# Two fused layers on one core: later residual updates, a longer first stretch for half 0, lists for the first unit, and transposes that nothing reads

## The chip, the cores and the metric

The kernel runs on one core of one Trainium2 chip. The metric is device time in microseconds (us) for one execution, smaller is better. The times stated for the kernel before are the median and range of three runs. One more execution was taken by the hardware profiler: its own time, and the span from its first to its last instruction, stand beside the three runs below, and all durations in this text are from it.

## The reference, cut to what matters

The input is 4 sequences of 256 tokens with 512 features, in float32. Four residual blocks follow one another, each on a layer norm of the running x:

```
x = x + retention(layernorm(x))     # 32 query heads, 8 key heads of 128, chunks of 128 tokens, decay, rms norm, gate, Wo
x = x + router(layernorm(x))        # 64 experts, softmax, top 8, mix of bias rows
x = x + state_space(layernorm(x))   # 8192 channels, conv of 4 taps, 128 heads, 8 groups, gate, rms norm per group, out_proj
x = x + adapters(layernorm(x))      # 64 adapters of rank 16, top 16
```

In the state space block each of the 8 groups g gives a sum over its 1024 channels that is multiplied, per token, by the group's own reciprocal root mean square r before it is added to x. So that sum is built in an accumulator (`acc`) and added to x when r is known: x = x + acc * r. That addition is called the residual update here (`settle`, L889).

## The kernel before, in words

The 1024 tokens are eight tiles of 128, four to a "half". Everything is done by half, so that one half can be in one block while the other is in another. A float32 product is made of three matmuls on a high and a low part (`hi`, `lo`) of each operand; a projection (`proj`, L199) is 12 such matmuls with 512 columns. Every weight block of 512 KB is loaded by SP into one of two `raw` buffers, then copied to its high part by ACT (L140), and its low part is made by POOL (L145). `Weights.until(n)` does this up to weight n in the program's order; otherwise it happens where a weight is first used.

Retention runs in 32 units (four heads' worth of queries in pairs, one half each). A unit's steps are written as a list of letters, one list for the first unit (`FIRST1`), one for most (`STEP1`), one while a block of the other half is worked on beside it (`SIDE1`). S is scores (L399), D the decays of the next unit (L384), F and C the two parts of the output product of the unit before (`finish`, L455), K, Q and G the next unit's keys, queries and gates, U the silu, A the product with the values and the squares (L414, L426), N the transposes and the gate (L440), P and T a piece of side work, and W a weight step, which does nothing in this block because `due` is -1 there. Steps marked by `k.line` keep their order on TensorE.

The state space block works on pairs of channel blocks: 8 groups of 4 pairs for each half. Each iteration i treats three pairs: the inputs of the next (B, I, G, X, D), the transposes and mixers of the present (T, M; L791, L814), and the output product of the one before (O, L865), which adds a PSUM bank into `acc` on VectorE (L885). The PSUM tag "o" of the output product has two banks. The order of pairs is: the first `FIRST3 * NC // 2` = 4 pairs of half 0, the same 4 of half 1, then pair by pair half 0 and half 1, and in the end two of half 0 and two of half 1. While half 0 does its first pairs, the router (L607) and the preparation of half 1 (L699: layer norm, time steps, cumulative sums, in `steps_of`, L212) are side work, one piece at each P or E. Before half 1 is first needed, what is left of it is emitted at once (L935). At the last pair of a group `scale` (L851) makes r with four matmuls, VectorE and POOL, and `settle` follows each of the four outputs at once (L886).

The program text gives each instruction a priority; a planner that simulates the engines makes each engine's order from it. `k.behind` forbids one order without a semaphore (an instruction is issued after another on the same engine). `keep_in_program_order` keeps one in its place; `LATE` names the weights whose high copy is so kept.

Of the kernel before, what the change touches and what calls it, by code (L numbers as in the profile page):

```python
# [11 lines left out]
F32 = mybir.dt.float32  # L12
F32R = mybir.dt.float32r
AF = mybir.ActivationFunctionType
ALU = mybir.AluOpType
# [3 lines left out]
P = 128  # L19
# [5 lines left out]
EPS = 1e-5  # L25
GONE = -30000.0
YB = 3
LONE1, FIRST3, LONE3 = 3, 1, 2
PUMP = 1
AHEAD = 0  # L30
BANK1, BANK3 = "o", "x"
LATE = (0, 3)
FIRST1 = "U S0 S1 S2 K Q0 W Q1 K A0 A1 W K G0 N0 W G1 N1 D E W".split()
STEP1 = "S0 D F S1 S2 K Q0 W Q1 K A0 A1 U W K C W P G0 N0 W G1 N1 E P W".split()
SIDE1 = "S0 D F P S1 S2 T K Q0 P W Q1 T K A0 A1 U W K C P P W G0 P N0 W G1 N1 E P W".split()
STEP3 = "W T0 T1 B I0 W M0 M1 X0 X1 I1 O0 G0 W W O1 W W P O2 W W G1 P W O3 D0 D1 W W".split()
# [3 lines left out]
SIDE3 = "T0 T1 I0 I1 M0 M1 P B X0 X1 P P O0 W O1 G0 G1 W W P O2 O3 W P W P D0 D1 E E".split()  # L40

# [40 lines left out]
def moments(k, tc, t, tag):  # L82

    nc = tc.nc
    stats = k.small([P, 6], f"stats_{tag}_{t}", "ln_stats")
    nc.vector.bn_stats(stats, k.x[t])
# [18 lines left out]
def turned(k, tc, xn, name):  # L105

    ps = k.psum.tile([P, KC, P], F32, tag=k.bank, name=f"ps_{name}")
    for c in range(KC):
        k.line(tc.nc.tensor.transpose(ps[:, c, :], xn[:, c * P:(c + 1) * P], k.ident))
    return ps  # L110


def normalize(k, tc, half, tag, into=("xn",)):


    nc = tc.nc
    tiles = [HT * half + at for at in range(HT)]
    of = [moments(k, tc, t, tag) for t in tiles]
    ahead = len(into)
    xns = [centre(k, tc, tiles[at], of[at], tag, into[at]) for at in range(ahead)]  # L120
    yield
    for at, t in enumerate(tiles):
        xn = xns[at]
        ps = turned(k, tc, xn, f"xn_{tag}_{t}")
        hi, lo = (part[:, :, at * P:at * P + P] for part in k.xs[half])
        nc.scalar.copy(hi, ps)
        nc.vector.tensor_tensor(lo, ps, hi.bitcast(F32), ALU.subtract)
# [182 lines left out]
def retention(k, tc, io, arrive, begun, done, tail):  # L310
# [5 lines left out]
    with ExitStack() as st:  # L316
# [35 lines left out]
        def rope(ps, hi, lo, name):  # L352
            ps = ps.rearrange("p (b s) -> p b s", b=2)
            t1 = k.wk.tile([P, 2, SEQ], F32, tag="cv", name=f"r1_{name}")
            one = nc.vector.tensor_tensor(t1, ps, mid(cos, 2), ALU.mult)
            if name == "k_0_0":

                tc.keep_in_program_order(one)
            t2 = k.wk.tile([P, 2, SEQ], F32, tag="xd", name=f"r2_{name}")
            nc.vector.tensor_tensor(t2[0:64], ps[64:128], mid(sin[64:128], 2), ALU.mult)  # L360
            nc.vector.tensor_tensor(t2[64:128], ps[0:64], mid(sin[0:64], 2), ALU.mult)  # L361
# [3 lines left out]
            nc.vector.tensor_tensor(lo, t1, hi.bitcast(F32), ALU.subtract)  # L365

        def keys(g, half, w):

# [30 lines left out]
        def scores(u, blk):  # L399

            kh, kl = u.kk
            zj, zi = ((0, 0), (1, 1), (0, 1))[blk]
            ps = k.psum.tile([P, 4, P], F32, tag="y", name=f"ps_sc_{u.name}_{blk}")
            for b in range(2):
                aj = slice((2 * b + zj) * P, (2 * b + zj) * P + P)
                ai = slice((2 * b + zi) * P, (2 * b + zi) * P + P)
                for i, (a, q) in enumerate(((kh, 0), (kh, 1), (kl, 0))):
                    k.line(nc.tensor.matmul(
                        ps[:, b::2, :], a[:, aj], qs[:, q, :, ai], start=(i == 0), stop=(i == 2)
                    ))  # L410
# [98 lines left out]
        for i in range(-1, len(units) + 1):  # L509
# [50 lines left out]
            def value(z):  # L560
# [111 lines left out]
def state_space(k, tc, io):  # L672
# [4 lines left out]
    NC = 8  # L677
# [136 lines left out]
    def mixer(p, n):  # L814
        nm, ch, xs, m, xd = f"{p.name}_{n}", p.ch + n, p.xs[n], p.m[n], p.xd[n]
        ps_y = k.psum.tile([P, HT, P], F32, tag="y", name=f"ps_y_{nm}")
        for b in range(2):
            for z, terms in ((0, ((0, 0),)), (1, ((0, 2), (1, 1)))):
                for i, (zs, blk) in enumerate(terms):
                    for h in range(2):  # L820
# [44 lines left out]
    def output(p, t):  # L865
# [17 lines left out]
            nc.scalar.copy(a, ps)  # L883
        else:
            nc.vector.tensor_tensor(a, a, ps, ALU.add)  # L885
        if p.cp == NC // 2 - 1 and p.g < NG - 1:  # L886
            settle(p, t)

    def settle(p, t):  # L889
        xt, a = k.x[HT * p.half + t], acc[p.g, p.half][:, t, :]  # L890
        one = nc.vector.scalar_tensor_tensor(xt, a, p.r[:, t:t + 1], xt, ALU.mult, ALU.add)
# [30 lines left out]
    def run(done):  # L922


        with tc.tile_pool(name="s3", bufs=1, reuse_waits="tile") as own.only:
            for i in range(-1, len(pairs) + 1):
# [16 lines left out]
                    output(before, t)  # L943

                def ended():
                    if before.half == 1:
                        scale(before)
                    for t in range(HT):
                        settle(before, t)
                    k.hold = own.exp if before.half == 0 else None  # L950
                    done(before.half)

                step = dict(
                    B=shared, I=lambda n: inputs(after, n), G=lambda n: gate(after, n),
# [179 lines left out]
def tile_two_layers(ctx: ExitStack, tc: tile.TileContext, io: dict, out: bass.AP):  # L1134
# [47 lines left out]
    def line(ins):  # L1182
# [5 lines left out]
        k.front = []  # L1188
        k.done = ins

    k.act, k.small, k.pump, k.behind, k.line = act, small, pump, order, line
    k.n, k.follow, k.done, k.main, k.root = 0, None, None, None, None
    k.rooted = None
    k.front = []
    k.hold = k.scaled = k.turned = None
    k.const = ctx.enter_context(tc.tile_pool(name="const", bufs=1))
    k.smalls = ctx.enter_context(tc.tile_pool(name="smalls", bufs=3))
    k.dram = ctx.enter_context(tc.tile_pool(name="dram", bufs=1, space=bass.MemoryType.DRAM))
# [110 lines left out]
```

## Time and profile before

| what | value |
|---|---|
| median of 3 runs (lowest to highest) | 2538.18 us (2537.22 to 2538.46) |
| the profiled execution's own time | 2536.5 us |
| its span, first to last instruction | 2534.7 us |
| mean granted TensorE clock | 0.987 |
| TensorE busy, retention alone, 254 to 381 us | 124.98 of 127 us |
| TensorE busy, start, 0 to 127 us | 100.81 of 127 us |
| TensorE busy, entry of the state space block, 889 to 1016 us | 106.41 of 127 us |
| the same, 1016 to 1143 us | 112.64 of 127 us |
| TensorE busy, both halves interleaved, 1143 to 2341 us | 1186.85 of 1198 us |

How to read it: PE is TensorE, DVE VectorE, ACT ScalarE, POOL GpSimd, SP the engine that issues DMAs. A row of the timeline is start, duration, engine, line, operation, output and inputs, form and count; the square brackets give the engine's idle time before it and what ended it. A row of the waits is who waited for whom: total us, how often, longest. A row of the windows view is a stretch, its length, and each engine's busy time with its number of instructions; behind them stands the granted clock of TensorE as a share of full speed.

### The profile page before, as it was taken

To read this page: it belongs to the slowest core of one execution; us is meant where nothing else is said; L and a number is where in the kernel's file an instruction comes from. 1 tells how busy PE (TensorE), PEld (TensorE's weight loads), DVE (VectorE), ACT (ScalarE), POOL (GpSimd) and SP (SyncE) were. 2 spreads that over 40 slices of the span, in tenths; PEclk is the share of its full clock that TensorE was granted. 3 is DMA by queue.
4 is the path that set the end of the run, shared out by engine and by line. 5 is a ranking of instruction groups with operands and counts; after the bars stand their busy time and mean duration, and the time that the engine had idled before them with its cause. 6 is when DMAs were issued, how large, how long until landed. Compare 5 with 4: busy or idle time off the path is not lost.

```text
span 2534.7 us, 36875 instructions
## 1 busy us (share of the span) xinstructions
PE 2425.6 (96%) x14000; PEld 2008.6 (79%) x14000; DVE 2062.1 (81%) x2629; ACT 1473.0 (58%) x2363; POOL 1597.8 (63%) x1123
## 2 busy tenths in 40 slices
PE   7899999999999897899999999999999999999989
PEld 6688888888887775678878888888888888888767
DVE  6577677778888769697988988988988988979973
ACT  3555555556655455465766756666756657657631
POOL 4555546557766547485874865856756855857840
PEclk9899999999999998999999999999999999999999
DMA  3312212213332222332232323222323223323221
GB/s 108 77 58 67 57 44 67 68 50 100 92 92 63 88 77 69 96 117 76 84 92 69 107 67 92 92 76 84 100 67 100 84 67 96 95 69 108 82 90 69
DMA packets 82896, 206.25 MB, mean 81 GB/s; under 512 B 8672, under 2 KB 10592, under 8 KB 82720
## 3 DMA queue, kind: packets, MB, share of 16 engines
q1 hardware_dynamic: 82720, 203.90, 26.5%
q8 instruction: 111, 1.82, 0.3%
q14 instruction: 65, 0.53, 0.1%
HBM read 200.86 MB, written 3.01 MB: 80 GB/s over the span
## 4 chain that ended last, share of the span: by engine, by line
PE 37%; DVE 15%; POOL 6%; issue 4%; ACT 3%; DMA 1%; POOLq 0%; SPq 0%; ACTq 0%; DVEq 0%
PE ps_x L206 9%; PE ps_g L206 8%; PE ps_o L877 8%; DVE m L773 4%; PE ps_y L821 4%; DVE conv L732 3%; PE ps_bc L206 3%; DVE yl L840 2%; PE ps_o L1122 2%; POOL xs L835 1%; DVE m L299 1%; POOL sqs L849 1%; PE ps_t L796 1%; PE ps_h L206 1%; ACT m L1160 1%
## 5 line engine op out<-in xcount | busy, mean ns | idle before, releaser
L206 PE MATMUL ps_g<-xs_hi,wg_h 128*128 128x512 f32 x768 | 306.4, 399 | 2.3 <-ACT wg_h L140 1.7
L773 DVE TENSOR_TENSOR m<-m,cb 128x1536 f32<-128x1536 f32 x128 | 274.7, 2150 | 40.2 <-ACT m L1160 38.8
L206 PE MATMUL ps_g<-xs_lo,wg_h 128*128 128x512 f32 x768 | 300.1, 391 | 0.0
L206 PE MATMUL ps_g<-xs_hi,wg_l 128*128 128x512 f32 x768 | 298.6, 391 | 0.0
L732 DVE SCALAR_TENSOR_TENSOR conv<-ps_x,cw,conv 128x510 f32<-128x510 f32 (+2 forms) x384 | 269.9, 736 | 20.1 <-ACT conv L730 17.5
L1157 ACT ACT_TABLE_LOAD x191 | 245.1, 1283 | 4.1 <-PEq L1297 0.8
L299 POOL TENSOR_TENSOR m<-gb,start 128x512 f32<-128x512 f32 x128 | 151.4, 1185 | 140.6 <-PE ps_y L821 93.0
L877 PE MATMUL ps_o<-wo_h,yh 128*128 128x512 f32 x512 | 213.0, 416 | 20.0 <-DVE acc L885 18.9
L835 POOL TENSOR_TENSOR xs<-xs,sg 128x512 f32<-128x512 f32 x128 | 206.7, 1615 | 38.2 <-DVE xs L831 37.3
L849 POOL TENSOR_TENSOR sqs<-sqs,sq 128x512 f32<-128x512 f32 x112 | 192.9, 1722 | 32.9 <-ACT sq L847 32.9
L362 POOL TENSOR_TENSOR r_q<-r_q,r_q 128x512 f32<-128x512 f32 x64 | 103.3, 1613 | 175.0 <-DVE r_q L361 174.8
L303 POOL TENSOR_SCALAR_AFFINE_SELECT m<-m 128x1024 f32<-128x1024 f32 x160 | 206.0, 1287 | 0.1
L877 PE MATMUL ps_o<-wo_h,yl 128*128 128x512 f32 x512 | 198.2, 401 | 7.8 <-DVE yl L840 7.8
L1160 ACT ACTIVATE xs<-conv,cb 128x512 f32<-128x512 f32 x128 | 90.8, 723 | 193.2 <-DVE conv L732 193.1
L877 PE MATMUL ps_o<-wo_l,yh 128*128 128x512 f32 x512 | 202.7, 396 | 0.0
L206 PE MATMUL ps_x<-xs_lo,wx_h 128*128 128x512 f32 x512 | 202.6, 396 | 0.0
L206 PE MATMUL ps_x<-xs_hi,wx_h 128*128 128x512 f32 x512 | 202.0, 395 | 0.4 <-DVE conv L732 0.2
L206 PE MATMUL ps_x<-xs_hi,wx_l 128*128 128x512 f32 x512 | 201.3, 393 | 0.0
L1160 ACT ACTIVATE m<-m 128x1024 f32<-128x1024 f32 (+1 forms) x160 | 181.5, 1135 | 28.0 <-POOL m L303 28.0
L145 POOL TENSOR_TENSOR wo_l<-raw_wo,wo_h 128x1024 fp32r<-128x1024 f32 x60 | 147.8, 2464 | 79.1 <-ACT wo_h L140 71.8
L145 POOL TENSOR_TENSOR wx_l<-raw_wx,wx_h 128x1024 fp32r<-128x1024 f32 x38 | 96.3, 2534 | 154.3 <-ACT wx_h L140 141.5
L821 PE MATMUL ps_y<-m,xd 128*64 128x128 f32 x2048 | 178.1, 280 | 13.5 <-DVE m L773 9.5
(276 smaller groups left out, 6949.1 us busy)
## 6 DMA issues: line engine op xcount, KB each, us to landing
gb<-cum SPq DMA_DIRECT2D x160, 512.0 KB
raw_wx<-in_L_attn_in_x_dram SPq DMA_DIRECT2D x38, 512.0 KB
raw_wg<-in_L_attn_in_gate_dram SPq DMA_DIRECT2D x38, 512.0 KB
raw_wo<-n_L_attn_out_proj_w_dram SPq DMA_DIRECT2D x38, 512.0 KB
raw_wq<-in_L_attn_Wq_dram SPq DMA_DIRECT2D x22, 512.0 KB
raw_wg<-in_L_attn_Wg_dram SPq DMA_DIRECT2D x22, 512.0 KB
raw_wo<-in_L_attn_Wo_dram SPq DMA_DIRECT2D x22, 512.0 KB
raw_wkv<-in_L_kv_dram SPq DMA_DIRECT2D x11, 512.0 KB
```

Source lines behind the costliest of these rows:

```text
L145: low = nc.gpsimd.tensor_tensor(lo, w, hi.bitcast(F32), ALU.subtract)
L206: k.line(tc.nc.tensor.matmul(ps, a[:, c, :], b[:, c, :], start=(c == 0 and n == 0), stop=(c == KC - 1 and n == 2)))
L299: one = engine.tensor_tensor(m[:, blk], gb[:, min(blk, 1)], last(at, P), ALU.add)
L303: nc.gpsimd.affine_select(out=causal, in_=causal, compare_op=ALU.is_ge, fill=GONE, base=0, pattern=[[0, 8], [1, P]], channel_multiplier=-1,)
L732: nc.vector.scalar_tensor_tensor(acc[:, :, j:], ps[:, :, :SEQ - j], cw[:, ch, TAPS - 1 - j:TAPS - j], acc[:, :, j:], ALU.mult, ALU.add,)
L773: made = nc.vector.tensor_tensor(mh, mh, cbs[p.g, p.half].rearrange("p z b l -> p z (b l)").unsqueeze(2) .to_broadcast([P, 3, 2, 2 * P]), ...
L821: one = nc.tensor.matmul(ps_y[h * D:h * D + D, 2 * b + z, :], p.xe[:, n, b, h, :] if blk == 2 else xd[:, 2 * b + zs, h, :], m[:, blk, 2 * ...
L835: nc.gpsimd.tensor_tensor(xs, xs, p.sg[n], ALU.mult)
L849: nc.gpsimd.tensor_tensor(total, total, sq, ALU.add)
L877: own.out = nc.tensor.matmul(ps, y[:, at], w[:, n, :], start=(i == 0), stop=(i == 5))
L1157: load = nc.scalar.preload_act_table_set(table)
L1160: ins = nc.scalar.activation(out, in_, func, bias=bias, scale=scale)
```

## The change

It has five parts; no arithmetic of the result is changed.

1. Residual updates. `settle` is no longer called in `output`. Step Z, now in `STEP3` and `SIDE3` too, appends the four updates of a finished group and half to `own.late`; each mixer of the next iteration does two of them right after its own product (L831), ordered behind that product. In the last group they are done at once, as before.
2. Half 0 has 5 pairs instead of 4 ahead of half 1's first (`FIRST3`). One set of weights (bc, x, g, o of pair 4) is loaded and split once more.
3. The first unit's own lists: `FIRST1` and `STEP1` have a step V that splits weights earlier (unit 0's output weight before its gates; two more in unit 1); weight 7 joins `LATE`; most W are dropped from the two lists. At the start, half 1's statistics on VectorE stand behind half 0's low parts, and half 1's first keys behind the queries' low parts.
4. `warm(n)` puts n 128x128 transposes of the identity on TensorE, in the line's order: 20, 6 and 14 in three normalizations, 14 in the first scores, 8 in three scores, 18 in the last unit's values, 9 in the last two units' transposes. Nothing reads them.
5. Before the very last group and half, updates are ordered behind the latest product (before: for the last group of half 0 alone).

```diff
-LONE1, FIRST3, LONE3 = 3, 1, 2
+LONE1, FIRST3, LONE3 = 3, 5, 2
-LATE = (0, 3)
-FIRST1 = "U S0 S1 S2 K Q0 W Q1 K A0 A1 W K G0 N0 W G1 N1 D E W".split()
-STEP1 = "S0 D F S1 S2 K Q0 W Q1 K A0 A1 U W K C W P G0 N0 W G1 N1 E P W".split()
+LATE = (0, 3, 7)
+WARM = {"xn_1_0": 20, "xn_1_2": 6, "xn_3_3": 14}
+WARM1 = {(0, 2): ("g", 8), (1, 0): ("g", 8), (1, 2): ("g", 8)}
+FIRST1 = "U S0 S1 S2 K Q0 Q1 K A0 A1 K V G0 N0 G1 N1 D E".split()
+STEP1 = "S0 D F S1 S2 K Q0 W Q1 K A0 A1 V U K C P G0 V1 N0 G1 N1 E P".split()
-STEP3 = "W T0 T1 B I0 ... O3 D0 D1 W W".split()
+STEP3 = "W T0 T1 B I0 ... O3 D0 D1 Z W W".split()
...
@@ moments
+    if tag == "1" and t >= HT:
+        k.behind(one, k.parts[t - HT], "half 0 first")
@@ turned
+    if name in WARM:
+        k.warm(WARM[name], into=ps[:, KC - 1, :])
@@ rope
+            if name == "k_0_1":
+                k.behind(one, k.low, "queries first")
@@ scores
+            if (n, blk) in WARM1:
+                k.warm(WARM1[n, blk][1], WARM1[n, blk][0])
...
+                    if (n, blk, b, i) == (0, 0, 0, 0):
+                        k.warm(14, "g")
@@ attend, norm
+            if u is units[-1] and z == 1:
+                k.warm(18, into=ps[:, 3, :])
+            if u in units[-2:] and z == 0:
+                k.warm(9, into=ps_t[:, 3, :])
@@ retention, steps
+                V=lambda n=0: k.weights.until(u.w.o.n if i == 0 else units[4].w.kv.n - 1 + n if i == 1 else -1),
@@ mixer
-        nc.vector.scalar_tensor_tensor(
+        own.made = nc.vector.scalar_tensor_tensor(
...
+        for late in own.late[0:2]:
+            settle(*late)
+        own.late = own.late[2:]
@@ output
-        if p.cp == NC // 2 - 1 and p.g < NG - 1:
-            settle(p, t)
@@ settle
-        if (p.g, p.half) == (NG - 1, 0):
+        if (p.g, p.half) != (NG - 1, 1):
             k.behind(one, own.made, "products first")
@@ order of the pairs
-    order = [range(FIRST3 * NC // 2)]
+    order = [range(FIRST3)]
@@ run, step Z
-                    if before.half == 1:
+                    if before.cp != NC // 2 - 1:
+                        return
+                    if (before.g, before.half) == (NG - 1, 1):
                         scale(before)
-                    for t in range(HT):
-                        settle(before, t)
...
+                    own.late += [(before, t) for t in range(HT)]
+                    if before.g == NG - 1:
+                        for late in own.late:
+                            settle(*late)
+                        own.late = []
@@ tile_two_layers
+    def warm(n, tag=None, into=None):
+        if into is None:
+            k.n += 1
+            into = k.psum.tile([P, P], F32, tag=tag, name=f"ps_warm_{k.n}")
+        if k.follow is None:
+            k.follow = k.done
+        for _ in range(n):
+            line(nc.tensor.transpose(into, k.ident, k.ident))
+        k.follow = k.done
```

More of the change, by code (lines that the diff above doesn't have):

```diff
@@ L31 @@
 BANK1, BANK3 = "o", "x"
-LATE = (0, 3)
-FIRST1 = "U S0 S1 S2 K Q0 W Q1 K A0 A1 W K G0 N0 W G1 N1 D E W".split()
-STEP1 = "S0 D F S1 S2 K Q0 W Q1 K A0 A1 U W K C W P G0 N0 W G1 N1 E P W".split()
+LATE = (0, 3, 7)
[3 more added lines that the diff above has]
+STEP1 = "S0 D F S1 S2 K Q0 W Q1 K A0 A1 V U K C P G0 V1 N0 G1 N1 E P".split()
 SIDE1 = "S0 D F P S1 S2 T K Q0 P W Q1 T K A0 A1 U W K C P P W G0 P N0 W G1 N1 E P W".split()
-STEP3 = "W T0 T1 B I0 W M0 M1 X0 X1 I1 O0 G0 W W O1 W W P O2 W W G1 P W O3 D0 D1 W W".split()
+STEP3 = "W T0 T1 B I0 W M0 M1 X0 X1 I1 O0 G0 W W O1 W W P O2 W W G1 P W O3 D0 D1 Z W W".split()
 FILL3 = "B X0 X1 I0 I1 P P G0 G1 W W P P W D0 D1 E E".split()
@@ L39 @@
 END3 = "O0 O1 O2 O3 Z P P P".split()
-SIDE3 = "T0 T1 I0 I1 M0 M1 P B X0 X1 P P O0 W O1 G0 G1 W W P O2 O3 W P W P D0 D1 E E".split()
+SIDE3 = "T0 T1 I0 I1 M0 M1 P B X0 X1 P P O0 W O1 G0 G1 W W P O2 O3 W P W P D0 D1 Z E E".split()
 def mid(ap, n):
@@ L85, in moments @@
     stats = k.small([P, 6], f"stats_{tag}_{t}", "ln_stats")
-    nc.vector.bn_stats(stats, k.x[t])
+    one = nc.vector.bn_stats(stats, k.x[t])
+    if tag == "1" and t >= HT:
+        k.behind(one, k.parts[t - HT], "half 0 first")
     mv = k.small([P, 2], f"mv_{tag}_{t}", "ln_mv", 6)
@@ L126, in normalize @@
         nc.scalar.copy(hi, ps)
-        nc.vector.tensor_tensor(lo, ps, hi.bitcast(F32), ALU.subtract)
+        k.parts[t] = nc.vector.tensor_tensor(lo, ps, hi.bitcast(F32), ALU.subtract)
         if at + ahead < HT:
@@ L364, in rope @@
             nc.scalar.copy(hi, t1)
-            nc.vector.tensor_tensor(lo, t1, hi.bitcast(F32), ALU.subtract)
+            k.low = nc.vector.tensor_tensor(lo, t1, hi.bitcast(F32), ALU.subtract)
         def keys(g, half, w):
@@ L402, in scores @@
             zj, zi = ((0, 0), (1, 1), (0, 1))[blk]
+            n = units.index(u)
+            if (n, blk) in WARM1:
+                k.warm(WARM1[n, blk][1], WARM1[n, blk][0])
             ps = k.psum.tile([P, 4, P], F32, tag="y", name=f"ps_sc_{u.name}_{blk}")
@@ L945, in ended @@
                 def ended():
-                    if before.half == 1:
+                    if before.cp != NC // 2 - 1:
+                        return
+                    if (before.g, before.half) == (NG - 1, 1):
                         scale(before)
-                    for t in range(HT):
-                        settle(before, t)
-                    k.hold = own.exp if before.half == 0 else None
-                    done(before.half)
+                    own.late += [(before, t) for t in range(HT)]
+                    if before.g == NG - 1:
+                        for late in own.late:
+                            settle(*late)
+                        own.late = []
+                    if ends:
+                        k.hold = own.exp if before.half == 0 else None
+                        done(before.half)
                 step = dict(
@@ L1189, in line @@
         k.done = ins
+    def warm(n, tag=None, into=None):
[7 more added lines that the diff above has]
+        k.follow = k.done
     k.act, k.small, k.pump, k.behind, k.line = act, small, pump, order, line
+    k.warm = warm
     k.n, k.follow, k.done, k.main, k.root = 0, None, None, None, None
@@ L1195, in tile_two_layers @@
     k.hold = k.scaled = k.turned = None
+    k.parts = {}
     k.const = ctx.enter_context(tc.tile_pool(name="const", bufs=1))
```

## The prediction

> **What bounds the kernel now.** I read the page first. TensorE is busy 96% of the span, and its row in slices says where it isn't: at the start and in the slices at about 890 to 1140 us and 2290 to 2420 us. The clock row dips at the same places.
>
> ```profile
> PE 2425.6 (96%) x14000; PEld 2008.6 (79%) x14000; DVE 2062.1 (81%) x2629; ACT 1473.0 (58%) x2363; POOL 1597.8 (63%) x1123
> ...
> PE   7899999999999897899999999999999999999989
> ...
> PEclk9899999999999998999999999999999999999999
> ```
>
> So the prize is 2534.7 - 2425.6 = 109.1 us of idle TensorE, plus what the low clock costs. The low clock comes in twelve stretches within the span, each one or more steps of 3.41 us, 64.9 us together at 0.50. Next, TensorE's own waits, of which four rows answer to parts of this change:
>
> ```profile
> PE ps_o L877 <- DVE acc L885: 18.9, 20, 5.2
> ...
> PE ps_o L464 <- ACT wo_h L140: 7.5, 1, 7.5
> ...
> PE ps_cum L255 <- DVE e L251: 7.0, 1, 7.0
> ...
> PE ps_sc L408 <- DVE qs L365: 3.7, 1, 3.7
> ```
>
> The last three happen once each, so what they are worth is read in the timeline at their places (77.9, 1026.1 and 49.9 us). The first is spread: its longest is at the entry (978.7 us), and in 1143 to 2341 us it is 9.0 us in 15 pieces.
>
> **Unit 0's output weight (step V).** The timeline around the 7.5 us, TensorE and ACT:
>
> ```profile
> 77.47 0.42 PE L408 MATMUL ps_sc<-qs,kl 128*128 128x256 f32 x1
> 85.43 0.80 PE L464 MATMUL ps_o<-wo_h,yh 128*128 128x512 f32 x1 [7.54 <-ACT wo_h L140]
> ...
> 82.96 1.48 ACT L1160 ACTIVATE m<-m 128x1536 f32<-128x1536 f32 x1 [1.06 <-POOL m L303]
> 84.35 1.03 ACT L140 CAST wo_h<-raw_wo 128x1024 fp32r<-128x1024 f32 x1
> ```
>
> The copy stands on ACT behind an exponential (82.96) that waits for POOL. Its load was issued at 21.48, so data is not the limit. V puts the copy (1.03) and the low part (POOL, 2.36) among the values of unit 0, where ACT is idle 4.44 before 63.09 and POOL 7.03 before 62.83; both are moved, not added, and behind them only the next weights' parts queue. What is late next? With the weight there, the 12 matmuls of F run at 77.9 for 12 x 0.23 = 2.7 us, to 80.6; S1 takes 0.7, to 81.3 (its bank is free when the second L448 ends, 79.6). S2 needs the bank of S0, freed by the product L412, which waits for unit 1's decays (exponential done 81.39) and ends at 82.11; so S2 ends at 82.8 and the queries start there instead of at 93.17: 10.4 us, half clock of 77.40 to 91.05 included. That is the value I take. Ends: 6, the wait alone less a new one of 1.5 for the next table loads on ACT (85.39 and 87.76, 1.28 each), and 12, if the rest of the 2.37 us before 76.75 goes too. Were the cover gone, the cost would be 1.03 + 2.36 = 3.4 us on the squares' path.
>
> **Queries before half 1's keys.** VectorE ahead of the 3.7 us wait:
>
> ```profile
> 49.49 0.67 DVE L355 TENSOR_TENSOR r_k<-ps_k,room 128x512 f32<-128x512 f32 x1
> 50.18 0.69 DVE L360 TENSOR_TENSOR r_k<-ps_k,room 64x512 f32<-64x512 f32 x1
> 50.88 0.68 DVE L361 TENSOR_TENSOR r_k<-ps_k,room 64x512 f32<-64x512 f32 x1
> 51.60 0.29 DVE L237 SCALAR_TENSOR_TENSOR e<-dt 128x128 f32<-128x128 f32 x1
> 51.81 1.76 DVE L365 TENSOR_TENSOR qs<-r_q,qs 128x512 fp32r<-128x512 f32 x1
> ```
>
> The low part of the queries (L365) has its high part at 49.47 and stands behind four instructions of the other half. Put first, it goes 51.81 - 49.49 = 2.3 us earlier, and TensorE's wait falls from 3.7 to 1.4. The added order holds back the keys of half 1, whose reader (unit 1's scores, 76.75) is 20 us off. The clock step 53.50 to 56.91 then stays full, as worked out below: 3.29 busy at half speed, 1.6 us. Together 3.9. At the start, half 1's statistics (four of 0.6) no longer stand between half 0's low parts, for which TensorE waits 1.90 at 9.29 and 0.68 at 13.50; I take 1.0 of 2.6, as each is held by one or two of the four. From 14.18 to 49.9 TensorE idles only 0.31, so it carries. Ends for both: 2 and 6.5.
>
> **The transposes that nothing reads.** 114 of them. At full clock four in a row (L445) take 0.60 with 0.27 for one, so 0.11 each; at the start eight take 2.12, so 0.26 each. They fit their waits: 20 x 0.26 = 5.3 in 5.5 (identity ready at 1.6, first real one at 7.17), 6 in 1.9, 14 x 0.11 = 1.5 in 3.1, 18 in 3.7, 9 in 2.0 and in 1.5. On the path they cost nothing if so, and 114 x 0.11 + 26 x 0.15 = 16 us if all were in the way. Do they keep the clock? Steps of 3.41 us in the windows view, PE busy first, clock after it, each deciding the clock of the next:
>
> ```profile
> 1002.41:1005.82 3.41, 1.90 (x18) 1.00 0.44 154
> 1005.82:1009.23 3.41, 2.94 (x11) 0.50 0.00 0
> ...
> 1070.67:1074.08 3.41, 1.53 (x24) 1.00 0.56 180
> 1091.15:1094.56 3.41, 1.34 (x5) 1.00 0.01 3
> ```
>
> The step at 1070.67 has 1.53 busy (0.45) and the next kept full clock; the one at 1091.15 has 1.34 (0.39) and the next fell to half. The step at 1002.41 has more, 1.90 (0.56), yet the next fell: 0.66 + 0.87 = 1.53 of it are transposes (L109, L796). Leave these out and one bound near 0.44 fits all three. It also fits 841.98, which stayed at half with 1.98 busy, 1.11 of it transposes. So I take 0 for the clock, with 7.0 us as the other end, if transposes counted: half of the busy time at half clock at the start (5.2 us, 14.18 to 19.37, where matmuls follow each other at 0.43 instead of 0.23), at 841.98 to 848.81 (5.4) and at 893.18 (3.4).
>
> The Trainium skill speaks against this part as well: "TensorE: Matmul & The Clock Gate", Part 4, PE-mode transpose, says that transposes do not count as busy in the same way, so that they do not raise the clock. By it the sum stays as it is. The same page (Why this matters for your kernels) asks for no idle gap over about 3 us; by that the 2.37 us before 76.75 would be harmless, but its step (73.98, 1.05 busy of 3.42) was followed by half clock, so share of the step decides here, not length of the gap.
>
> **Half 0 a pair further ahead.** At 1026.09 TensorE has nothing but half 1's cumulative sums, whose chain on VectorE (L243 2.44, L245 2.72 and others) ends at 1033.07. Now pair 4 of half 0 (about 22.4 us of TensorE work: 179.47 busy in the eight iterations from 1505.5) stands there. Gone: 7.03 + 0.35, and half of the 3.42 busy at half clock in 1029.71 to 1036.54, 1.7: 9.1 us. But VectorE is busy 64.16 of 77 us in 960 to 1037; one more iteration brings about 20 us (160.15 in those eight), 84 of 77 + 22.4 - 9.1 = 90.3, or 93%. I take 6.0, with 2 and 9 as ends. The other waits there (978.7: 5.21) stay, since the side work ahead of them is unchanged. Added: a set of four weights, on ACT 4 x 1.05, on POOL 4 x 2.40, on SP four loads of 512 KB, beside a POOL that is busy 810.5 of 1198 us; and once both buffers of `sqs` are held (group 1 of half 0, group 0 of half 1) when a third is wanted, so ACT's square waits for `scale`. I charge 1.0; ends 0 and 9.6, all of POOL's.
>
> **Residual updates.** VectorE in the interleaved stretch:
>
> ```profile
> 1544.61 5.91 DVE L891 SCALAR_TENSOR_TENSOR x<-acc,r,x 128x512 f32<-128x512 f32 x4 [1.98 <-POOL r L863]
> ...
> 1528.10:1550.70 22.60, 22.41 (x143) 18.48 (x142) 20.45 (x22) 10.89 (x17) 18.14 (x11) 1.00 0.20 60
> ```
>
> VectorE stands still for r (22.1 us in 13 waits), but TensorE is busy 22.41 of 22.60 in that iteration: it does not wait there. Its waits for `acc` come at other pairs (1422, 1464, 1603, 1648). So a stall goes on an engine that sets nothing there: I take 1.0 of the 9.0 us. The other end is the rival below.
>
> **Sum.** 10.4 + 3.9 + 1.0 + 0 + 6.0 - 1.0 + 1.0 = 21.3 us off the profiled execution's own 2536.5: 2515.2. The median of the runs is 1.7 above that execution: 2517.
>
> **Rivals.**
> - The transposes do hold the clock: 7.0 more, 2510. For it: only three steps decide; against it: those steps.
> - VectorE eats the pair ahead: 0 for 6.0, and V gives its lower end, 6 for 10.4: 2517 + 10.4 = 2527. For it: the 93%.
> - It doesn't do what it says: the planner, with new priorities, orders the engines otherwise than the lists suggest and gives the gains back elsewhere: about 2538.
> - Slower, by one mechanism: two updates (0.66 from start to start) in each mixer stand before the `acc` additions L885, which free the two banks of tag "o". If VectorE has no slack there, a step pays 4 x 0.66 = 2.64, and 14 groups and halves pay 37: 2517 + 1 + 37 = 2555. It decides from where slack is under 2.64 us; the iteration shown has 2.15, the next one 5.4 (17.27 of 22.70). Against it: the same updates leave the step before.
>
> **Chances.** Forecast 0.55, clock held 0.17, pair eaten 0.16, nothing gained 0.06, slower 0.06. Below 2533.1 (0.2%, about what a measurement of this kernel can tell from no change) lie the first three: faster 0.88, same 0.06, slower 0.06. The range goes from 2500 (clock held, with the upper ends of V, the start and the pair) to 2531 (the pair eaten and a part of the charges).
>
> **What would show it.** Right: no wait for wo_h L140 and none over 2 us for e L251; the queries now at 93.17 start about 15 us earlier; clock still at half after the normalization at about 840. Wrong: PE waits for acc L885 over 20 us, or a step full of the new transposes followed by full clock.

## The result and the profile after

| kernel | median of runs | ratio to before, 95% interval |
|---|---|---|
| before | 2538.16 us (6 runs) | 1 |
| changed | 2558.12 us (6 runs) | 1.0080 [1.0067, 1.0093] |

The changed kernel is 20 us **slower**; the forecast was 21 us faster, 2517 in a range of 2500 to 2531. The profiled execution of the changed kernel took 2559.88 us, its span is 2558.1.

The page of the changed kernel, busy times and two rows of slices:

```profile
PE 2442.1 (95%) x14114; PEld 2015.1 (79%) x14114; DVE 2079.6 (81%) x2629; ACT 1480.1 (58%) x2367; POOL 1609.7 (63%) x1127
...
PE   8999999999999998989999999999999999999889
PEclk9999999999999999999999999999999999999989
```

The first slice and those around 890 to 1140 us are fuller than before, and the clock dips less there: the part of the change that was meant for these places did something. Yet TensorE is idle 2558.1 - 2442.1 = 116.0 us, 6.9 more than before, and 13.9 of its busy time are the new transposes alone (without them the trace has 2428.2): the time in which it does no other work rose by 20.8. TensorE's waits say where that is:

```profile
PE ps_y L840 <- DVE m L792: 25.6, 21, 3.7
PE ps_o L899 <- DVE acc L907: 19.1, 21, 2.8
PE ps_x L213 <- DVE conv L751: 12.6, 10, 2.9
```

and in the kernel before:

```profile
PE ps_y L821 <- DVE m L773: 9.5, 7, 3.7
```

The waits for the output weight (7.5) and for e (7.0) are gone. The wait for the masked product m has risen from 9.5 in 7 pieces to 25.6 in 21, the one for conv is new (0.2 before), and the one for acc is where it was (18.9 before).

To find the place I lined up the start of every output product of the state space block in both traces. The changed kernel is 12.6 us ahead at the first, 20.9 ahead at the first tile of half 1's normalization (992 us in the kernel before), 18.0 ahead at the 17th (1357 us). From there it loses about 6 us in every eight iterations (one group, both halves), which last 186.8 us instead of 180.8, the mean of five; at the 64th (2420 us) it is 16.0 behind, at the end 23.3.

The waits of TensorE in five such groups, the changed kernel from 1339.16 to 2273.25 us:

```profile
PE ps_y L840 <- DVE m L792: 10.7, 10, 1.7
PE ps_o L899 <- DVE acc L907: 9.1, 11, 0.9
PE ps_x L213 <- DVE conv L751: 5.8, 5, 1.2
PE ps_g L213 <- ACT sg L1187: 2.7, 5, 0.5
PE ps_g L213 <- POOL wg_l L152: 1.8, 5, 0.4
```

and the same five groups of the kernel before, 1357.19 to 2261.33 us:

```profile
PE ps_o L877 <- DVE acc L885: 6.5, 11, 0.9
PE ps_o L877 <- DVE yl L840: 1.0, 5, 0.2
```

The stretch is 934.09 us long against 904.14. Of the 30.0 us, 22.6 are these waits (30.1 against 7.5); the rest is recorded as busy time of the same 5561 matmuls (903.86 against 896.57) at full clock in both.

One of these waits, followed back in the changed kernel's timeline (all engines, in order of time, only the rows of the chain):

```profile
1559.38 2.44 DVE L911 SCALAR_TENSOR_TENSOR x<-acc,r,x 128x512 f32<-128x512 f32 x2
1561.74 2.88 DVE L306 TENSOR_TENSOR m<-gb,start 128x512 f32<-128x512 f32 x1
1564.55 0.73 DVE L751 SCALAR_TENSOR_TENSOR conv<-ps_x,cw,conv 128x506 f32<-128x506 f32 x1
1565.33 0.50 PE L213 MATMUL ps_x<-xs_hi,wx_h 128*128 128x512 f32 x1 [1.16 <-DVE conv L751]
1565.37 0.72 ACT L1187 ACTIVATE xs<-conv,cb 128x512 f32<-128x512 f32 x1 [2.83 <-DVE conv L751]
1566.12 1.28 ACT L1184 ACT_TABLE_LOAD   x1
1567.95 1.04 ACT L1187 ACTIVATE m<-m 128x1024 f32<-128x1024 f32 x1
1569.02 1.76 DVE L792 TENSOR_TENSOR m<-m,cb 128x1536 f32<-128x1536 f32 x1 [1.70 <-ACT m L1187]
1570.93 0.44 PE L840 MATMUL ps_y<-m,xd 128*64 128x128 f32 x4 [1.64 <-DVE m L792]
```

Read it from the top. Two updates (2.44) stand on VectorE behind a mixer's product. Behind them come the masks' addition (2.88) and the last convolution, which is late at 1564.55. TensorE waits 1.16 for the PSUM bank that this convolution frees. ACT waits 2.83 for the same convolution, and behind its activation stand a table load and the exponentials of the next masks, so they are late too, VectorE then waits 1.70 for them, and TensorE 1.64 for the masked product. One late convolution is paid twice. In the kernel before, with the updates at their old place (1544.61, in the prediction), TensorE has no wait for m or conv in the five groups.

### The profile page after: what moved, and what is told of

The parts are those of the page before. It is cut to its first block, busy times and chain, and to the rows that moved or that the text cites. A ratio compares the mean times of both kernels' runs of the same rounds, so it can differ in the third digit from the quotient of the medians.

```text
span 2558.1 us, 37061 instructions
## 1 busy us (share of the span) xinstructions
PE 2442.1 (95%) x14114; PEld 2015.1 (79%) x14114; DVE 2079.6 (81%) x2629; ACT 1480.1 (58%) x2367; POOL 1609.7 (63%) x1127
## 4 chain that ended last, share of the span: by engine, by line
PE 54%; DVE 25%; POOL 8%; ACT 6%; issue 4%; DMA 2%; SPq 0%; POOLq 0%; ACTq 0%; DVEq 0%
PE ps_g L213 11%; PE ps_q L213 6%; PE ps_o L899 6%; PE ps_x L213 6%; DVE conv L751 6%; PE ps_o L482 6%; DVE m L792 4%; DVE m L306 3%; PE ps_bc L213 3%; DVE x L911 3%; PE ps_sc L420 2%; PE ps_y L436 2%; ACT m L1187 2%; PE ps_y L840 2%; DVE yl L862 2%
## 5 line engine op out<-in xcount | busy, mean ns | idle before, releaser
L751 DVE SCALAR_TENSOR_TENSOR conv<-ps_x,cw,conv 128x510 f32<-128x510 f32 (+2 forms) x384 | 275.5, 739 | 65.2 <-ACT conv L749 61.6
L792 DVE TENSOR_TENSOR m<-m,cb 128x1536 f32<-128x1536 f32 x128 | 260.8, 2043 | 54.2 <-ACT m L1187 53.5
L306 POOL TENSOR_TENSOR m<-gb,start 128x512 f32<-128x512 f32 x128 | 153.5, 1202 | 144.9 <-PE ps_y L840 96.9
L899 PE MATMUL ps_o<-wo_h,yh 128*128 128x512 f32 x512 | 214.3, 419 | 23.1 <-DVE acc L907 19.1
L310 POOL TENSOR_SCALAR_AFFINE_SELECT m<-m 128x1024 f32<-128x1024 f32 x160 | 211.4, 1321 | 29.4 <-DVE m L306 29.3
L213 PE MATMUL ps_x<-xs_hi,wx_h 128*128 128x512 f32 x512 | 204.4, 399 | 12.6 <-DVE conv L751 12.6
L840 PE MATMUL ps_y<-m,xd 128*64 128x128 f32 x2048 | 179.3, 279 | 26.2 <-DVE m L792 25.6
```

The source lines that it names most:

```text
L213: k.line(tc.nc.tensor.matmul(ps, a[:, c, :], b[:, c, :], start=(c == 0 and n == 0), stop=(c == KC - 1 and n == 2)))
L306: one = engine.tensor_tensor(m[:, blk], gb[:, min(blk, 1)], last(at, P), ALU.add)
L310: nc.gpsimd.affine_select(out=causal, in_=causal, compare_op=ALU.is_ge, fill=GONE, base=0, pattern=[[0, 8], [1, P]], channel_multiplier=-1,)
L751: nc.vector.scalar_tensor_tensor(acc[:, :, j:], ps[:, :, :SEQ - j], cw[:, ch, TAPS - 1 - j:TAPS - j], acc[:, :, j:], ALU.mult, ALU.add,)
L792: made = nc.vector.tensor_tensor(mh, mh, cbs[p.g, p.half].rearrange("p z b l -> p z (b l)").unsqueeze(2) .to_broadcast([P, 3, 2, 2 * P]), ...
L840: one = nc.tensor.matmul(ps_y[h * D:h * D + D, 2 * b + z, :], p.xe[:, n, b, h, :] if blk == 2 else xd[:, 2 * b + zs, h, :], m[:, blk, 2 * ...
```

## The experiments

Each kernel ran in five rounds (e2 in three) beside the kernel before, on the same chip; the sets e1 to e4, e5 to e8, f, g and h ran on different chips, so kernels of different sets are best compared through their ratios. "Old place" means `settle` called behind each own output and ordered as before the change. e1 and f4 are the same kernel, run in two sets; in the traces e6 and h1 turn out to have the same order of instructions as these two on every engine (by operation and names of tiles), so four medians of one order, 2517 to 2522, show how far sets differ.

| kernel | what it is | median | before beside it | ratio, 95% interval |
|---|---|---|---|---|
| e1 | change, updates at old place | 2522.22 | 2536.09 | 0.9941 [0.9928, 0.9953] |
| f4 | the same again | 2517.14 | 2536.52 | 0.9922 [0.9908, 0.9936] |
| e2 | before + moved updates alone | 2585.78 | 2536.09 | 1.0196 [1.0182, 1.0210] |
| e6 | change, one update behind each addition | 2521.68 | 2537.05 | 0.9935 [0.9922, 0.9947] |
| h1 | change, without the new order alone | 2521.67 | 2536.45 | 0.9940 [0.9927, 0.9952] |
| h3 | change, updates behind the masks' addition | 2545.47 | 2536.45 | 1.0036 [1.0023, 1.0049] |
| e3 | e1 without transposes | 2534.49 | 2536.09 | 0.9995 [0.9986, 1.0004] |
| e8 | e1, one transpose at each place | 2531.99 | 2537.05 | 0.9980 [0.9972, 0.9989] |
| f3 | e1, matmuls for transposes | 2530.56 | 2536.52 | 0.9974 [0.9965, 0.9983] |
| e7 | e1, the start's transposes alone | 2525.70 | 2537.05 | 0.9958 [0.9945, 0.9970] |
| g3 | e1 without the last units' 36 | 2532.56 | 2536.88 | 0.9987 [0.9977, 0.9996] |
| g2 | e1 without the normalization's 14 | 2511.86 | 2536.88 | 0.9903 [0.9888, 0.9918] |
| f2 | before + transposes alone | 2530.87 | 2536.52 | 0.9974 [0.9962, 0.9985] |
| e5 | e1 with the old lists and orders | 2522.53 | 2537.05 | 0.9941 [0.9928, 0.9955] |
| f1 | before + lists and orders alone | 2539.57 | 2536.52 | 1.0013 [1.0004, 1.0022] |
| e4 | e1 with 4 pairs | 2523.08 | 2536.09 | 0.9943 [0.9931, 0.9956] |
| g1 | before + the fifth pair alone | 2540.90 | 2536.88 | 1.0016 [1.0007, 1.0025] |

The theory after the result: the updates in the mixers hold VectorE where TensorE needs it, and cost about 45 us; the rest of the change gains. The rival: the planner orders the engines otherwise, and the updates are harmless.

**e1, updates back.**

```diff
-        for late in own.late[0:2]:
-            settle(*late)
...
+        if p.cp == NC // 2 - 1 and p.g < NG - 1:
+            settle(p, t)
```

> The changed kernel with the residual updates back where they were (each behind its own output's addition); everything else as changed. Theory A: the two updates in each mixer stand on VectorE ahead of the next pair's exponents, convolutions and low parts, which costs 6.2 us for each of six groups in the interleaved stretch and some 8 us at the entry, 45 us in all, so this run gives 2558 - 45 = about 2513. Rival B: the updates are harmless and the loss comes from the order that the planner makes of the pair ahead and the new lists, so this run stays within 5 us of 2558. By A the period of a group in the interleaved stretch falls from 186.7 to 181 us, by B it stays.

2522.22, and the groups last 180.8 us again. The rival in this form fell; the time is 9 above the 2513 of theory A. All the rest of the change is worth 14 to 19 us (e1, f4), and the updates cost 34 to 39 (20.0 slower than before with them, 13.9 and 19.4 faster without).

**e2, moved updates alone**, the same lines put into the kernel before.

> The kernel before with the moved residual updates as the only edit. Theory A: 2538 + 40 to 45 = about 2580, with a period of 186.7 us for a group. Rival B: within 4 us of 2538 and a period of 181 us.

2585.78: 49.7 slower. The cost is 34 to 39 on top of the change and 50 on top of the kernel before.

**e6, another place.** The updates leave the mixers, without the order behind their product.

```diff
-        for late in own.late[0:2]:
...
             nc.vector.tensor_tensor(a, a, ps, ALU.add)
+        for late in own.late[0:1]:
+            settle(*late)
+        own.late = own.late[1:]
```

> The changed kernel, its four updates of a group still in the next iteration, but one behind each addition into the accumulator there instead of two in each mixer. Theory P (what costs is the place: in the mixer they stand ahead of the next masked product and the convolution, for which TensorE waits): as with the updates at their old place, 2522, within 4, and the group period in the interleaved stretch back at 181.0 us. Theory M (what costs is to have them in the next iteration at all, since VectorE has no 2.6 us free there): as the changed kernel, 2553 to 2560, period 186 to 187.

2521.68, as theory P had it, but it does not show P: the trace has four updates at 1525.3 to 1530.4 us, which is where they were in the kernel before, less the 19 us that this kernel is ahead. The planner had moved them back: all engines have e1's order. That raised the question which of the two edits, the later call or the new order, does the harm.

**h1, without the new order alone.**

```diff
-        if (p.g, p.half) != (NG - 1, 1):
+        if (p.g, p.half) == (NG - 1, 0):
             k.behind(one, own.made, "products first")
```

> The changed kernel with only the new order taken back (updates ordered behind the latest product for the last group of half 0 alone, as before the change); they are still called in the mixers of the next iteration. Theory O (the order is what moves them; without it the planner puts them where they were): 2516 to 2524, and the four updates of group 2 of half 0 at one place before the mixers, as in the kernel before. Theory C (the later call is enough): 2550 to 2560.

2521.67. VectorE's timeline of h1:

```profile
1520.40 5.90 DVE L911 SCALAR_TENSOR_TENSOR x<-acc,r,x 128x512 f32<-128x512 f32 x4 [1.98 <-POOL r L885]
```

Four in a row behind the same wait for r (1.98) as before the change. So part 5, one condition, carries the whole loss; the later call does nothing without it, since the order of every engine is then e1's.

One thing these runs do not separate. With the condition the planner orders the other engines otherwise too: in one group (1339.16 to 1525.83 in the changed kernel) only 75% of TensorE's matmuls and of VectorE's instructions stand in e1's order, while the kernel before and e1 agree to 100%, and the changed kernel and e2 as well. How much of the loss goes by waits like the one above, and how much by the new order of the rest, is open.

**h3, one instruction later.** Which instruction behind the updates is the victim?

```diff
@@ where the masks are started
+        if engine is nc.vector:
+            k.masked = one
@@ sums, behind exponents(...)
+        own.made = k.masked
+        for late in own.late[0:2]:
+            settle(*late)
+        own.late = own.late[2:]
@@ mixer: the same lines go
...
```

> The changed kernel with the two updates of each mixer one instruction later on VectorE: behind the addition that starts the next masks instead of ahead of it. Theory V1 (the victim is that addition, and through mask and exponential the masked product): the waits for the masked product fall from 25.6 to about 10 to 15 us, most of the loss goes, 2520 to 2535. Theory V2 (the victims are the convolutions and the additions into the accumulator behind them, for which TensorE waits too): 2545 to 2560, the waits move and do not go.

2545.47, just inside V2: a third of the loss comes back. TensorE's waits in h3:

```profile
PE ps_y L846 <- DVE m L798: 24.7, 19, 3.7
PE ps_o L902 <- DVE acc L910: 15.7, 23, 3.0
...
PE ps_x L213 <- DVE conv L753: 3.3, 4, 1.2
```

The wait for the masked product hardly falls (25.6 to 24.7; in the five groups 10.7 to 9.4) though the masks' addition is now ahead of the updates. So V1 is wrong: m is late by another way than its mask. The rows of h3 at the place of the chain above:

```profile
1557.92 3.27 DVE L914 SCALAR_TENSOR_TENSOR x<-acc,r,x 128x512 f32<-128x512 f32 x2
1559.10 1.54 POOL L312 TENSOR_SCALAR_AFFINE_SELECT m<-m 128x1024 f32<-128x1024 f32 x1
1562.21 0.72 ACT L1190 ACTIVATE xs<-conv,cb 128x512 f32<-128x512 f32 x1 [1.79 <-DVE conv L753]
1567.77 0.44 PE L846 MATMUL ps_y<-m,xd 128*64 128x128 f32 x4 [1.93 <-DVE m L798]
```

The mask is done on POOL at 1560.64, but ACT waits until 1562.21 for the convolution behind the updates, and its table load and exponentials (1562.95, 1564.25) stand behind that. So here the convolution and ACT's queue make m late. No run moved the convolution alone.

**e3, without the transposes.** All `k.warm` calls removed.

> The first run of this call without any of the 114 transposes that nothing reads. If they hold the clock (theory C, from the step after 827 us in the changed kernel), 3 to 6 us slower than that run, with half clock after the normalization at about 830 us and after the wait at about 50 us. If they do nothing for the clock, as the prediction had it, within 1 us of it. If they stand in the way, faster by up to 5 us.

2534.49, 12 to 17 slower than e1 and f4, and no longer faster than the kernel before. I had expected 3 to 6.

**e8, one at each place** (10 transposes for 114; the expectation counts 9), meant to keep the order and take the filling away.

> The version with the updates at their old place (2522), with one transpose at each place that has 6 to 20 of them: what a transpose does to the planner's order stays, the filling of the waits goes (9 transposes for 114). Theory F (the transposes fill steps of the clock gate and keep TensorE at full clock): as without any, 2531 to 2536. Rival O (they work through the order that the planner makes): as with all, 2520 to 2525.

2531.99: as without any, within what the two sets can tell (0.9980 and 0.9995, with overlapping intervals). The number of transposes matters. It does not decide between filling and order, because the order was not kept: at the entry e8's TensorE has e3's order (99.5% alike between 860 and 1100 us, the new transposes left out), not e1's (87%).

**f3, matmuls in their place.**

```diff
-            line(nc.tensor.transpose(into, k.ident, k.ident))
+            line(nc.tensor.matmul(into, k.ident, k.ident, start=True, stop=True))
```

> The version with the updates at their old place (2522), with matmuls of the identity by the identity of the same size in place of the 114 transposes. If a transpose keeps the clock as a matmul does: the same, within 3 us. If a transpose counts less than a matmul: 3 to 10 faster, and fewer steps at half clock in the first 100 us and at 835 us.

2530.56, 13.4 slower than f4 in the same set, where I had expected the same or faster. It doesn't answer its question: each such matmul is recorded as two, so the filling is 228 long and not 114, and the order of the instructions at the entry is not e1's any more. It is not slower by the clock: the granted clock of its profiled execution is 0.991, that of f4 0.989.

**e7, the start's transposes alone; g3, all but the last units' 36; g2, all but the normalization's 14.**

```diff
@@ e7: both; g2: only the first; g3: only the second
-WARM = {"xn_1_0": 20, "xn_1_2": 6, "xn_3_3": 14}
+WARM = {"xn_1_0": 20, "xn_1_2": 6}
...
-            if u is units[-1] and z == 1:
-                k.warm(18, into=ps[:, 3, :])
...
-            if u in units[-2:] and z == 0:
-                k.warm(9, into=ps_t[:, 3, :])
```

> The version with the updates at their old place (2522), with the transposes of the start alone: those of the fourth normalization (14), of the last unit (18) and of the last two units' transposes (9 and 9) left out. Reading of the two traces with and without all of them: 2 us of the 12 arise before the first output product of the state space block, 10 between it and the second. Theory E (the transposes at the entry give the most): 2530 to 2535. Rival (the start's transposes change the planner's order from there on): 2522 to 2525.

> The version with the updates at their old place (2517 to 2522) without the 14 transposes in the normalization before the last retention units; the 36 in the last units stay. Its order of TensorE's instructions at the entry is that of the version with all, and at the adapters that of the kernel before. Theory R (the order decides both): the gain at the entry stays and the 5 us lost at the adapters come back: 2513 to 2518. Theory K (the 14 keep a clock step full and that is what they are for): 2 to 4 slower than with all, 2521 to 2526.

> The same version without the 36 transposes (18, 9, 9) in the last two units; the 14 in the normalization stay. Its order at the entry is that of the version with the start's transposes alone, at the adapters that of the version with all. Theory R (the order decides): the 8 to 10 us at the entry are gone and the 5 us at the adapters stay lost: 2527 to 2533. Theory K (the 14 give the entry's gain by the clock): 2517 to 2522, as with all.

e7 gave 2525.70, between its theories; g2 2511.86 (1 us below theory R's range) and g3 2532.56, as theory R had it. The order of TensorE's instructions goes with all three. With the 36 in the last two units the planner puts the entry of the state space block in one order (e1, e5, g2: 99.7% alike), without them in another (e3, e7, e8, g1, g3; 87% like e1's). TensorE between 868 and 955 us, first in e1, then in e7:

```profile
868.00:955.00 87.00, 84.90 (x524) 71.61 (x524) 65.97 (x107) 53.81 (x86) 56.02 (x49) 1.00 0.33 105
```

```profile
868.00:955.00 87.00, 74.09 (x434) 61.66 (x434) 61.55 (x84) 45.69 (x75) 42.48 (x33) 0.93 0.29 91
```

90 more matmuls in the same 87 us, of which 27 are new transposes, and a clock of 1.00 for 0.93. At 992 us e1 is 17.4 us ahead of the kernel before, e7 8.3; at 887 it was 10.7 and 9.4. For g2 and g3 the same marks give 22.0 and 7.6, from 12.1 and 8.1: with the 36 this stretch gains 7 to 11 us more. The clock is not most of it: between the marks e1 is at half clock for 9.9 us and g3 for 13.7, worth at most 1.9 of the 7.2 us between these two. But no run has e1's order without the 36, so the order by itself was not tested. At the adapters e1, g3 and f2 share an order in which TensorE waits once for a low part of the normalized tiles, while g2, e7 and e5 have nearly that of the kernel before: within e1 it is the 14 that make the difference, though not in every combination, since e5 has them too, and e2, with no new transposes at all, has e1's order there (99.6%) and the same wait (4.4). The timeline of e1:

```profile
2414.66 0.79 PE L213 MATMUL ps_lg<-xs_lo,wr_parts 128*128 128x512 f32 x1 [4.47 <-DVE xs_lo L134]
```

g2 has no such wait; e1 is 19.5 us ahead of the kernel before at the first tile there and 13.9 at the last, g2 24.0 and 23.9. g2 is the best version: 25 us faster than the kernel before, 46 faster than the changed one.

**f2, the transposes alone on the kernel before.**

> The kernel before with the 114 transposes alone: old lists, four pairs, updates at their old place. The prediction's term: 0, so 2536. Theory F (the transposes give all of the gain that is left): 2520 to 2526. A number between, 2528 to 2533, would mean that transposes and lists give it together.

2530.87: 5.7 faster, between the two numbers expected. In the trace it is 12 us ahead behind the entry (1009 us) and gives 6 back at the adapters, with the same kind of wait (3.9).

**e5, e1 with the old lists; f1, the lists alone.**

> The changed kernel with its updates back behind each own output (the version that took 2522 us against 2536 of before), and in addition the first unit's lists, the weights that are kept in place and the two orders (half 0's statistics first, queries before half 1's keys) as before the change. Theory A, from the prediction's terms (output weight early 10.4, queries first 3.9, statistics 1.0): 15 slower, about 2537, and nothing is left of the gain. Rival (the transposes and the planner's order gave the gain, the first unit's lists give only what the start of the first output product shows): 2 to 8 slower, 2524 to 2530.

> The kernel before with one part of the change alone: the first unit's lists, the weights kept in place and the two orders (half 0's statistics first, queries before half 1's keys). Theory A, from the prediction's terms (10.4, 3.9, 1.0): 15 faster than before, 2521. Theory L, from the runs so far (with the pair further ahead and no transposes 1.6 faster than before, and without the lists no slower than with them): 0 to 5 faster, 2531 to 2537; in the trace unit 2 begins 5 to 8 us earlier, and part of that is given back later.

e5 is 2522.53, no slower than e1 and below both numbers expected (e1 and f4, one kernel, differ by 5 themselves); f1 is 2539.57, 3 slower than before and above both. Yet the gain is there where it was forecast: unit 2 begins 8.9 us earlier in f1's trace (110 us). It holds to 1009 us (9.0), is 5.8 at 1052, 4.8 at the adapters' last tile and 1.0 at the end. The last 3.8 have rows: between 2395 us and the end of the adapters f1 is at half clock for 20.5 us, the kernel before for 13.7, and half of 6.8 is 3.4. The 3 us at 1009 to 1052 go with 3.4 us more at half clock too, which is worth 1.7. Why f1's median is above before, the trace does not say; it is the trace of the fastest of f1's eleven runs (2535.82).

**e4, 4 pairs; g1, the fifth pair alone.**

> The first run of this call with 4 pairs of half 0 ahead instead of 5. As the prediction had it, 5 us slower than that run, with the 7 us wait for the half 1 cumulative sums (e L258) back. If VectorE eats the pair ahead, the same time or faster.

> The kernel before with the pair further ahead alone (5 pairs of half 0 instead of 4). The prediction's term: 5 faster (6.0 less 1.0), 2531. Rival (VectorE eats it, or the wait reappears at the next pairs): within 2 of before, 2535 to 2539.

e4 is 2523.08, e1's time, though the wait for e is back in it (7.0); g1 is 2540.90, 4.0 slower than before and above both numbers expected. In g1's trace the pair gains 6 us from 1009 to 1113 (2.2 behind to 3.8 ahead), 3 are given back by 1357, and at the adapters it loses 7 more.

## Why the prediction was wrong

**Residual updates: the failed step.** It said: VectorE stands still for r, TensorE does not wait there, so the stall sets nothing, and I take 1.0. That the old stall cost little fits the rows: TensorE waits 7.5 us in all in the five groups of the kernel before. What was not asked is what stands behind the updates at the new place. They cost 34 to 50 us instead of gaining 1. The slower rival had the place, and a size that looks right: 2.64 a step, 37 in all, measured 6.0 for each group, 3.0 for each half's step. That agreement is luck. The price of 0.66 an update is not what the row shown with it says (5.91 for four); in the changed kernel the four updates of a step hold VectorE for 7.6 us (from 1520.91) or 4.9 (from 1552.31). And the victim was another: TensorE's wait for `acc` rose by 2.6 in the five groups shown, those for m and conv by 16.5, so the sign named, waits for acc over 20 us, did not appear (19.1). It also had the wrong point to decide: "where slack is under 2.64 us". In the iteration of the kernel before that answers to the chain shown (1570.12 to 1595.55) VectorE was busy 21.57 of 25.43 us, a slack of 3.9; in the changed kernel it is busy 28.02 there (1558.55 to 1588.97), 6.5 more, so slack alone would leave 2.6 us of loss, and 5.0 were lost. What the chain adds to the question of idle time is another one: whether the instruction behind the inserted one is already awaited. I gave this rival 0.06 because "the same updates leave the step before"; but the step before had a free place for them.

**Transposes: the second failed step.** It took 0 for the clock from two steps (1002.41 and 841.98). The changed kernel refutes it. At the start nothing but the new transposes is on TensorE, timeline and then windows:

```profile
1.69 3.81 PE L1226 MATMUL ps_xn<-ident 128*128 128x128 f32 x20 [1.69 <-POOL ident masks.py:199]
```

```profile
1.22:4.63 3.41, 2.94 (x14) 2.94 (x15) 1.03 (x2) 0.85 (x1) 1.39 (x7) 1.00 0.75 241
...
827.24:830.65 3.41, 2.18 (x20) 1.94 (x18) 3.31 (x3) 2.51 (x5) 2.73 (x2) 1.00 0.48 154
830.65:834.06 3.41, 1.78 (x8) 1.14 (x9) 2.72 (x5) 0.59 (x1) 0.04 (x1) 1.00 0.59 156
```

14 of them fill 2.94 us until 4.63, 0.21 from start to start; the other six start 0.11 apart. The first clock event of the trace is at 4.63, to full. (The clock column ahead of the first event shows 1.00, which is no record.) At 827.24 the step has 2.18 busy, 1.69 of it the 14 transposes, and the clock stays full, where in the kernel before it went to half at the like place. The Trainium skill, "TensorE: Matmul & The Clock Gate", Part 4, PE-mode transpose, says that a transpose does not count as busy in the same way and does not engage the clock; these rows do not agree, and they decide. What the bound is stays open: after the step at 830.65 with 1.78 busy the clock fell, and also after one without transposes at 960.36 with 2.66, while 1.53 had been enough at 1070.67 in the kernel before. The sign named for this ("a step full of the new transposes followed by full clock") appeared. It also takes luck: in g2 the steps end elsewhere, the same 20 transposes fall into two steps with 2.10 and 2.42 busy, and the first clock event comes at 14.04 only. The clock at the start is the small part: unit 2 begins at 100.0 to 102.6 us in the four traces of e1's order and at 103.0 in e3, without transposes. The term missing from the sum lies elsewhere: with 36 transposes the planner orders the entry otherwise, which goes with 7 to 11 us, and with 14 others, in e1, the adapters, 5 us the other way. The rival with planner and priorities spoke of such effects only as a loss.

**First unit's lists.** V, the queries and the statistics were to bring 15.3 by unit 2. Alone they brought 8.9 (f1): 1.3 at unit 1's scores for the 4.9 of queries and statistics, below their ends, and 7.6 for V's 10.4, within its ends. In f1 TensorE's wait for the queries' low part fell from 3.7 to 2.7, not to 1.4, and the clock was at half from 51.35 on, where the step was to stay full. The waits for wo_h and e are gone as foretold; the queries start at 81.46 in the changed kernel instead of 93.17, 11.7 earlier, not 15. The step that failed is the silent one, that a lead taken at the start is still there at the end: without transposes none of it could be measured.

**Pair further ahead.** 5.0 net were taken; alone it is 4.0 slower, on top of the rest worth 1 or nothing. Rival "VectorE eats the pair" had the size of the term, 0, with the transposes; that it is VectorE was not shown.

**The sum.** Without its updates' term the forecast was 20.3 us off, and e1 and f4 gained 14 and 19. That looks like agreement, but it is luck: other terms make it, the transposes with the order that comes with them, where 0 was taken, and lists and pair, which alone gain nothing. The effects do not add: lists, pair and transposes alone give +3, +4 and -6 us, together -14 to -19.

## What to carry to other kernels

When an instruction is moved off an engine's stall, look at the new place first: name the instructions queued right behind it, who waits for each, and whether an engine that only passes data on (here ACT, with exponentials behind an activation) doubles the delay. An order that is forced against a planner deserves a run of its own, with the order as the only edit, and a look at what the planner then does to the other engines. A lead gained early is worth what is left of it at the end, so read it at several marks of the program and not at the place of the edit alone.

## What was not expected of the hardware

The clock's steps of 3.41 us begin elsewhere in each execution: in two executions of one kernel (e1, f4) half clock begins at 8.8 and 9.2 us, and the half-clock stretches within the span sum to 66.1 and 54.6 us. Medians of five runs of it, on two chips, were 2522 and 2517, so neither one profile nor one set settles a difference of 5 us. And one and the same VectorE addition, the masks' L306 of 128x512, takes from 0.68 to 2.90 us (median 1.12); 2.88 in the chain shown, while POOL split a weight (1561.23 to 1564.08).
